# Hybrid layer on one core: where a new group's masked scores stand in TensorE's order

## The chip, the cores and the metric

The kernel runs on one core of a Trainium2 chip, as one launch. The metric is the time of one execution on the device in microseconds (us), as the median of the runs of a kernel. TensorE is called PE here, VectorE DVE, ScalarE ACT, GpSimd POOL and SyncE SP, as in the profile.

## The reference, cut to what matters

A layer with 1024 tokens (four batches of 256) and a width of 512: attention with an adapter, a clustered feed-forward layer, a state-space mixer and the feed-forward layer again, each on a layer-normalised input and added to the running `x`. The change lies in the mixer, which takes most of the time. It has 128 heads of 64 in eight groups of 16 heads:

```python
proj = input_states @ in_proj_w.T            # gate, then x, B, C, then dt
xBC = silu(causal_conv4(xBC) + conv_b)       # depthwise, four taps
dt = softplus(dt + dt_bias)
cum = cumsum(dt * A)
scores = (C @ B^T) * exp(cum_i - cum_j) * dt_j     # j <= i, heads of a group share B and C
y = scores @ x + D * x
g = y * silu(gate)
out = (g / rms of g over its group) * norm_w @ out_w.T
```

The products `C @ B^T` depend on the group and the batch only. They are computed and masked once for each group, and the 16 heads of the group multiply them with their own decay.

## The kernel before, in words

Channels lie on the 128 partitions, tokens along the free dimension. A block is 128 channels, which is two heads; there are 64 blocks, eight to a group. `block(i, ...)` (line 1175) is called once for each. Every product with weights is done as three matmuls on split operands (`mm3`, lines 110 to 117), so a projection of one block (1024 tokens) is two halves of 12 matmuls each, `projected` (line 1127), which calls `between` after the first half. What a block does:

- It projects its x channels into a PSUM tile `pp` and convolves them (`conv`, line 961): one scaling on ACT, three taps on DVE (line 971) that read PSUM, a SiLU on ACT (line 975). The result is `x2`.
- It projects its gate channels (also `pp`), with other PE work between the two halves, and ACT takes their SiLU (`gt`, line 1208).
- `differences` (line 999) makes the decays `em` of its two heads on DVE, POOL and ACT; `turned` (line 1022) transposes `x2` on PE into `trx` and scales it on DVE into `xd`; `weighted` (line 1019) multiplies each `em` with the group's masked scores `gm` on DVE (line 1020).
- `inner_products(i - 1)` (line 1160) does the weighted values of the block before: 32 matmuls into `pyy` (`product`, line 1038), then `gated` (line 1051): two steps on DVE (lines 1054 and 1057), a store to DRAM (`spill`), a square on ACT and its sum over the group on POOL (line 1067).
- `outer` (line 1150) does 24 matmuls (`pog`) of the output product of the group before, on what `recall` (line 1097) has loaded back from `spill` and split; the first of a group also takes the root of the summed squares (`root`, line 1085). `out_weights` (line 1073), eight a group, load and split the output weights: half of a group's before the gate projection of its last block, half at that block's end.

With the sixth and the seventh block of a group the B and C channels of the next group are projected and convolved. The first block of a group calls `scores` (line 978), a generator: it allocates `gm`, and each further step does two matmuls of one batch into a PSUM tile `pg` and one masking step on DVE (line 991) from there into `gm`. In every group but the first, the first block's order on PE is: both halves of x's projection; half of the gate's; scores of batches 0 and 1; weighted values of the block before; scores of batches 2 and 3; the other half of the gate's.

```python
for b in range(B):
    pg = ps.tile([P, 3, P], F32, name="pg", tag="m")
    ...
    nc.vector.tensor_tensor(gm[:, b], pg, tri.rearrange("p (s i) -> p s i", s=3), ALU.mult)
    yield
```

The tag "m" in `ps` has two buffers, which `pg`, `trx`, `pog` and the roots' `pqs` take by turns. `pp` has two buffers, `pyy`, `gm` and `xd` one, `em` four.

What sets the order: from block 8 on, PE's instructions stand in the order of the program (`manual_schedule`, line 1231). For the other engines the compiler's scheduler fixes an order ahead of time, the program's order being the priority among what it holds to be ready; at run time each engine works its list from the front. Nearly all DMAs are issued by SP.

Of the kernel before, what the change touches and what calls it, by code (L numbers as in the profile page):

```python
# [21 lines left out]
B, L, C = 4, 256, 512  # L22
# [57 lines left out]
def hybrid_kernel(  # L80
# [12 lines left out]
    x = keep.tile([P, TT, C], F32, name="x")  # L93
# [692 lines left out]
    def mixer(feed, later):  # L786
        with ExitStack() as es, ExitStack() as inner:
# [25 lines left out]
            def prepare(i):  # L813

                for n in range(i, i + 3):
                    fetch(n)
                if i < NW and i not in pieces:
                    pieces[i] = [pw.tile([P, KC, P], F32R, name=f"w{j}", tag=f"w{j}") for j in range(2)]
                    split(pieces[i], raws.pop(i), nc.gpsimd if i < 18 else nc.vector)

            def project(w, pp, cols):
                mm3(pp[:, cols], [[v[:, k, :] for v in w] for k in range(KC)],
                    [[v[:, k, cols] for v in xs] for k in range(KC)])
# [137 lines left out]
            def conv(pp, ch, tag, bufs):  # L961

                acc = (po_ if tag == "gb" else p2).tile([P, NT], F32, name="acc", tag=tag, bufs=bufs)
                nc.scalar.activation(  # L964
                    acc, pp, AF.Identity, bias=cb_s[:, ch : ch + 1], scale=cw_s[:, ch, 3:4]
                )
                av = acc.rearrange("p (b t) -> p b t", b=B)
                pv = pp.rearrange("p (b t) -> p b t", b=B)
                for tap in range(3):
                    d = 3 - tap  # L970
                    nc.vector.scalar_tensor_tensor(  # L971
                        av[:, :, d:], pv[:, :, : L - d], cw_s[:, ch, tap : tap + 1], av[:, :, d:],
                        ALU.mult, ALU.add,
                    )
                silus.append(nc.scalar.activation(acc, acc, AF.Silu).ins)
                return acc

            def scores(bt, ct):

                gm = p2.tile([P, B, 3, P], F32, name="gm", tag="gm", bufs=1)  # L980
                yield gm
                for b in range(B):
                    pg = ps.tile([P, 3, P], F32, name="pg", tag="m")
                    k0, k1 = bt[:, b * L : b * L + P], bt[:, b * L + P : (b + 1) * L]
                    q1 = ct[:, b * L + P : (b + 1) * L]
                    nc.tensor.matmul(
                        pg[:, 0:2, :].rearrange("p s i -> p (s i)"), k0, ct[:, b * L : (b + 1) * L],
                        start=True, stop=True,
                    )
                    nc.tensor.matmul(pg[:, 2, :], k1, q1, start=True, stop=True)  # L990
                    nc.vector.tensor_tensor(gm[:, b], pg, tri.rearrange("p (s i) -> p s i", s=3), ALU.mult)
                    yield

            def rows(h):
                r = p2.tile([P, NT], F32, name="r", tag="r", bufs=2)
                load(r, cumd[h : h + 1, :].to_broadcast([P, NT]))
                return r
# [21 lines left out]
            def weighted(e, gm):  # L1019
                nc.vector.tensor_tensor(e, e, gm, ALU.mult)  # L1020
# [52 lines left out]
            def out_weights(g, k):  # L1073

                r = po_.tile([P, C], F32, name="wor", tag="wor", bufs=2)
                tc.keep_in_program_order(load(r, wout[g * GB + k]))
                n = g * GB + k
                w = [po_.tile([P, C], F32R, name=f"wo{j}", tag=f"wo{j}", bufs=GB) for j in range(2)]
                nc.scalar.activation(w[0], r, AF.Copy, scale=nw_s[:, n : n + 1])
                nc.vector.scalar_tensor_tensor(  # L1080
                    w[1], r, nw_s[:, n : n + 1], w[0].bitcast(F32), ALU.mult, ALU.subtract
                )
                return w
# [43 lines left out]
            def projected(kind, n, between=lambda: None):  # L1127
                i = at[kind, n]
                prepare(i + 1)
                prepare(i + 2)  # L1130
                w = pieces.pop(i)
                if i == 0:
                    return first[1]
                pp = (
                    ps_y.tile([P, NT], F32, name="pp", tag="pyy") if (kind, n) == ("g", 0)
                    else ps_p.tile([P, NT], F32, name="pp", tag="pp")
                )
                for half in range(2):
                    project(w, pp, slice(half * 512, half * 512 + 512))
                    if half == 0:  # L1140
                        between()
                return pp
# [3 lines left out]
            def convolved(kind, g):  # L1146
                at_ = NB if kind == "b" else NB + G
                group[kind] = conv(projected(kind, g), at_ + g, "gb", 3)

            def outer():  # L1150

                q, t, hl = recalled.pop(0)
                po = ps.tile([P, C], F32, name="pog", tag="m")
                for half in range(2):
                    partial(po, q, hl[half], half)
                if t == 0:
                    rgs[q] = root(sqs.pop(q))
                scaled(q, t, po)

            def inner_products(m):  # L1160
                px2, gt, xd, em = stage.pop(m)
                py = product(xd, em)
                sqs[m // GB] = gated(m, px2, gt, py, sqs.get(m // GB))
# [2 lines left out]
            convolved("c", 0)  # L1166
            scoring = scores(group["b"], group["c"])
            gm = next(scoring)
            for _ in scoring:
                pass  # L1170
            rr = {h: rows(h) for h in range(2)}
            stage, sqs, wos, rgs, todo = {}, {}, {}, {}, []
            recalled = []
            PER = {1: 1, 2: 2, 3: 1, 4: 1, 5: 1, 6: 1, 7: 1}
            def block(i, scoring, gm):
                g, gi = divmod(i, GB)
                x2 = conv(projected("x", i), i, "x2", 2)
                if gi == 0 and g:
                    scoring = scores(group["b"], group["c"])
                    gm = next(scoring)  # L1180
                    todo.extend((g - 1, t) for t in range(TT))


                late = gi < 2 and g > 0
                if not late:
                    if recalled:
                        outer()
                    if i:
                        inner_products(i - 1)
                    while recalled:  # L1190
                        outer()
                if gi == 7:
                    wos.setdefault(g, []).extend(out_weights(g, k) for k in range(4))

                def between():
                    if late:
                        if gi == 0:
                            next(scoring)
                            next(scoring)
                        inner_products(i - 1)  # L1200
                        while recalled:
                            outer()
                    for _ in scoring:
                        pass

                pp = projected("g", i, between)
                gt = p2.tile([P, NT], F32, name="gt", tag="gt", bufs=1)
                nc.scalar.activation(gt, pp, AF.Silu)
                em = []
                for h in (2 * i, 2 * i + 1):  # L1210
                    with tc.issue_after(silus[2]) if i == 0 else ExitStack():
                        em.append(differences(h, rr.pop(h)))
                    if h + 2 < H:
                        rr[h + 2] = rows(h + 2)
                xd = turned(i, x2)
                if gi in NEXT and g + 1 < G:
                    convolved(NEXT[gi], g + 1)
                for e in em:
                    weighted(e, gm)
                stage[i] = (x2, gt, xd, em)  # L1220
                for _ in range(PER.get(gi + 1, 0)):
                    if todo:
                        q, t = todo.pop(0)
                        recalled.append((q, t, [recall(q, t, half) for half in range(2)]))
                if gi == 7:
                    wos[g].extend(out_weights(g, k) for k in range(4, 8))
                return scoring, gm

            for i in range(GB):
                scoring, gm = block(i, scoring, gm)  # L1230
            with tc.manual_schedule(engines={nc.tensor.engine}):
                for i in range(GB, NB):
                    scoring, gm = block(i, scoring, gm)
# [50 lines left out]

    later = ExitStack()
    mixer(attention(later), later)


# [67 lines left out]
```

## Time and profile before

| what | value |
|---|---|
| median of 3 runs | 1885.23 us (1880.72 to 1886.87) |
| the profiled execution | 1886.09 us |
| its span, first to last instruction | 1884.3 us |
| PE busy | 1805.5 us |
| DVE busy | 1475.8 us |
| ACT busy | 1470.4 us |
| masking steps (line 991) | 32, 0.55 us each (median) |
| products with the masked scores (line 1020) | 128, 1.75 us each (median) |
| mean granted clock of PE | 0.987 |

A row of the page's groups or of the timeline gives a line of the kernel, the engine, the operation, what it writes and reads, and how often; a time in square brackets is how long the engine stood idle before it, and for whom. "L1044" is line 1044. The profile gives one execution, with its own time; the runs' median comes from others.

### The profile page before, as it was taken

To read this page: it belongs to the slowest core of one execution; us is meant where nothing else is said; L and a number is where in the kernel's file an instruction comes from. 1 tells how busy PE (TensorE), PEld (TensorE's weight loads), DVE (VectorE), ACT (ScalarE), POOL (GpSimd) and SP (SyncE) were. 2 spreads that over 40 slices of the span, in tenths; PEclk is the share of its full clock that TensorE was granted. 3 is DMA by queue.
4 is the path that set the end of the run, shared out by engine and by line. 5 is a ranking of instruction groups with operands and counts; after the bars stand their busy time and mean duration, and the time that the engine had idled before them with its cause. 6 is when DMAs were issued, how large, how long until landed. Compare 5 with 4: busy or idle time off the path is not lost.

```text
span 1884.3 us, 29891 instructions
## 1 busy us (share of the span) xinstructions
PE 1805.5 (96%) x10706; PEld 1454.6 (77%) x10706; DVE 1475.8 (78%) x2304; ACT 1470.4 (78%) x2883; POOL 385.5 (20%) x393
## 2 busy tenths in 40 slices
PE   8999988899989999999999999999999999999997
PEld 6777767677777887878778878887887788788876
DVE  5566667789998788878887888779877978787777
ACT  6666675379998788878988798889788978887754
POOL 6332230014411211111112111111211111121100
PEclk9999999999999999999999999999999999999999
DMA  4000000034555445544554455445444544554241
GB/s 144 1 1 1 22 15 19 31 101 157 196 168 174 134 146 168 184 146 143 182 157 147 139 181 166 160 134 185 154 145 163 174 146 145 167 175 150 98 134 50
DMA packets 152773, 240.35 MB, mean 128 GB/s; under 512 B 12464, under 2 KB 77616, under 8 KB 152624
## 3 DMA queue, kind: packets, MB, share of 16 engines
q1 hardware_dynamic: 152624, 238.44, 39.0%
q8 instruction: 84, 1.38, 0.3%
q14 instruction: 65, 0.53, 0.1%
HBM read 202.75 MB, written 35.65 MB: 127 GB/s over the span
## 4 chain that ended last, share of the span: by engine, by line
PE 73%; DVE 12%; ACT 8%; DMA 3%; issue 3%; POOL 1%; SPq 0%; DVEq 0%; ACTq 0%; POOLq 0%
PE pp L115 11%; PE pp L116 11%; PE pp L117 11%; PE pyy L1044 7%; PE pog L115 6%; PE pog L117 6%; PE pog L116 6%; PE trx L1027 2%; ACT e L477 2%; DVE em L1020 2%; DVE acc L971 1%; DMA wor<-in_wout_dram 1%; PE ptr L493 1%; PE pq L115 1%; PE pq L116 1%
## 5 line engine op out<-in xcount | busy, mean ns | idle before, releaser
L115 PE MATMUL pp<-mx,w 128*128 128x512 f32 (+1 forms) x1160 | 464.2, 400 | 3.1 <-DVE acc L971 1.1
L116 PE MATMUL pp<-mx,w 128*128 128x512 f32 (+1 forms) x1160 | 453.1, 391 | 0.0
L117 PE MATMUL pp<-mx,w 128*128 128x512 f32 (+1 forms) x1160 | 452.8, 390 | 0.0
L971 DVE SCALAR_TENSOR_TENSOR acc<-pp,cw_s,acc 128x1012 f32<-128x1012 f32 (+2 forms) x240 | 304.8, 1272 | 21.3 <-ACT acc L964 19.4
L1020 DVE TENSOR_TENSOR em<-em,gm 128x1536 f32<-128x1536 f32 x128 | 249.2, 1952 | 54.6 <-ACT em L1016 54.6
L115 PEld LDWEIGHTS pp<-mx,w 128*128 128x128 f32 x1160 | 219.5, 189 | 53.7 <-issue 7.5
L1008 POOL TENSOR_SCALAR_AFFINE_SELECT r<-r 128x512 f32<-128x512 f32 x128 | 105.5, 825 | 749.0 <-DMA r<-cumd 616.5
L117 PEld LDWEIGHTS pp<-mx,w 128*128 128x128 f32 x1160 | 219.1, 189 | 46.6 <-issue 0.7
L116 PEld LDWEIGHTS pp<-mx,w 128*128 128x128 f32 x1160 | 219.4, 189 | 41.1 <-issue 0.6
L1067 POOL TENSOR_TENSOR sq<-sq,acc 128x1024 f32<-128x1024 f32 x55 | 139.0, 2528 | 359.7 <-ACT acc L1066 359.7
L115 PE MATMUL pog<-wo,gh 128*128 128x512 f32 x512 | 201.7, 394 | 1.3 <-DVE x L1115 0.8
L116 PE MATMUL pog<-wo,gh 128*128 128x512 f32 x512 | 199.6, 390 | 0.0
L117 PE MATMUL pog<-wo,gh 128*128 128x512 f32 x512 | 199.4, 390 | 0.0
L1044 PE MATMUL pyy<-em,xd 128*64 128x128 f32 (+1 forms) x2048 | 183.7, 329 | 1.3 <-DVE em L1020 0.9
L1044 PEld LDWEIGHTS pyy<-em,xd 128*64 128x64 f32 x2048 | 130.2, 137 | 59.8 <-issue 20.1
L1013 ACT ACTIVATE em<-r,col_t 128x128 f32<-128x128 f32 x512 | 170.1, 390 | 4.2 <-DMA r<-cumd 2.8
L1016 ACT ACTIVATE em<-r,col_t 128x128 f32<-128x128 f32 x512 | 169.2, 389 | 0.3
L1004 DVE TENSOR_SCALAR em<-r,col_t 128x128 f32<-128x128 f32 x512 | 135.7, 318 | 21.8 <-PE pyy L1044 17.8
L108 DVE TENSOR_TENSOR w<-wr,w 128x512 fp32r<-128x512 f32 x126 | 91.2, 724 | 76.8 <-ACT w L107 76.7
L107 ACT CAST w<-wr 128x512 fp32r<-128x512 f32 x144 | 88.7, 616 | 60.2 <-PE pp L116 57.4
L107 ACT CAST gh<-gr 128x512 fp32r<-128x512 f32 (+1 forms) x128 | 77.7, 608 | 62.7 <-PE pog L116 56.6
L477 ACT ACTIVATE e<-sc,nmx 128x256 f32<-128x256 f32 (+1 forms) x256 | 104.2, 442 | 21.0 <-DVE nmx L471 20.9
(290 smaller groups left out, 3309.0 us busy)
## 6 DMA issues: line engine op xcount, KB each, us to landing
wr<-in_win_dram SPq DMA_DIRECT2D x287, 256.0 KB, 2.8
r<-cumd SPq DMA_DIRECT2D x128, 512.0 KB, 4.0
spill<-gb SPq DMA_DIRECT2D x63, 512.0 KB, 2.8
gr<-spill SPq DMA_DIRECT2D x120, 256.0 KB, 2.9
wor<-in_wout_dram SPq DMA_DIRECT2D x64, 256.0 KB, 3.2
out_dram<-x SPq DMA_DIRECT2D x8, 256.0 KB, 2.3
x<-in_x_dram SPq DMA_DIRECT2D x1, 1536.0 KB, 8.8
gr<-spill SPq DMA_DIRECT2D x8, 192.0 KB, 2.5
```

Of the source, the lines that this page charges most:

```text
L107: nc.scalar.copy(hl[0], v)
L115: nc.tensor.matmul(o, lh, rh, start=(first and k == 0), stop=False)
L116: nc.tensor.matmul(o, lh, rl, start=False, stop=False)
L117: nc.tensor.matmul(o, ll, rh, start=False, stop=(last and k == n - 1))
L477: nc.scalar.activation(es_[c][:, 2 * j + pr, :], sc[:, j, :], AF.Exp, bias=nm[:, j : j + 1], accum_out=rs[:, c, h : h + 1],)
L971: nc.vector.scalar_tensor_tensor(av[:, :, d:], pv[:, :, : L - d], cw_s[:, ch, tap : tap + 1], av[:, :, d:], ALU.mult, ALU.add,)
L1004: nc.vector.tensor_scalar(e[:, b, 2, :], rv[:, b, 1, :], col_t[:, h, b, 1:2], 0.0, ALU.subtract, ALU.min,)
L1013: nc.scalar.activation(e[:, b, 1, :], rv[:, b, 1, :], AF.Exp, bias=col_t[:, h, b, 2:3])
L1016: nc.scalar.activation(e[:, b, 0, :], rv[:, b, 0, :], AF.Exp, bias=col_t[:, h, b, 0:1])
L1020: nc.vector.tensor_tensor(e, e, gm, ALU.mult)
L1044: nc.tensor.matmul(py[d, b, k * P :], xd[:, 2 * b + k, d], es2[hh][:, b, 2 * k : 2 if k == 0 else 3, :].rearrange("p s i -> p (s i)"), sta ...
L1067: (nc.gpsimd if n < NB - 1 else nc.vector).tensor_tensor(sq, sq, x2, ALU.add)
```

## The change

The generator's steps are no longer all taken between the halves of the gate's projection. In the first block of a group (not the first group) `scores` is now called before x's projection; a new local function `scored` takes two of its steps. It is passed to x's projection, so that scores of batches 0 and 1 stand between its halves, and with that ahead of x's convolution in the program, and it is called again at the head of `between`, so that scores of batches 2 and 3 stand in front of the weighted values of the block before. The four steps of group 0 are taken as before, by count.

```diff
--- before.py
+++ after.py
@@ -1166,19 +1166,25 @@
             convolved("c", 0)
             scoring = scores(group["b"], group["c"])
             gm = next(scoring)
-            for _ in scoring:
-                pass
+            for _ in range(B):
+                next(scoring)
             rr = {h: rows(h) for h in range(2)}
             stage, sqs, wos, rgs, todo = {}, {}, {}, {}, []
             recalled = []
             PER = {1: 1, 2: 2, 3: 1, 4: 1, 5: 1, 6: 1, 7: 1}
             def block(i, scoring, gm):
                 g, gi = divmod(i, GB)
-                x2 = conv(projected("x", i), i, "x2", 2)
                 if gi == 0 and g:
                     scoring = scores(group["b"], group["c"])
                     gm = next(scoring)
                     todo.extend((g - 1, t) for t in range(TT))
+
+                def scored():
+
+                    for _ in range(2 if gi == 0 and g else 0):
+                        next(scoring)
+
+                x2 = conv(projected("x", i, scored), i, "x2", 2)
 
 
                 late = gi < 2 and g > 0
@@ -1193,15 +1199,11 @@
                     wos.setdefault(g, []).extend(out_weights(g, k) for k in range(4))
 
                 def between():
+                    scored()
                     if late:
-                        if gi == 0:
-                            next(scoring)
-                            next(scoring)
                         inner_products(i - 1)
                         while recalled:
                             outer()
-                    for _ in scoring:
-                        pass
 
                 pp = projected("g", i, between)
                 gt = p2.tile([P, NT], F32, name="gt", tag="gt", bufs=1)
```

## The prediction

> **What bounds the kernel now.** I read first the page's busy times, then TensorE's (PE's) waits, then the timeline round one group start, then busy sums by window.
>
> ```profile
> span 1884.3 us, 29891 instructions
> ...
> PE 1805.5 (96%) x10706; PEld 1454.6 (77%) x10706; DVE 1475.8 (78%) x2304; ACT 1470.4 (78%) x2883; POOL 385.5 (20%) x393
> ```
>
> PE is busy in nearly all of the span. Summed over the stretch from 520 to 1700 us, its gaps of over 0.1 us come to only 18.7 us. PE's waits say whose they are (us in total, times, longest):
>
> ```profile
> PE pg L986 <- DVE gm L991: 14.4, 7, 4.6
> ...
> PE trx L1027 <- DVE gm L991: 2.1, 5, 1.0
> ...
> PE trx L1027 <- ACT rg L1093: 1.4, 1, 1.4
> ...
> PE trx L1027 <- DVE x L1115: 1.2, 4, 0.4
> ```
>
> Nearly all of it is one wait, seven times, once at each of the groups 1 to 7: the third batch's scores need a PSUM slot of the tag "m", which has two, and VectorE (DVE) has not yet masked the first batch's scores. PE's timeline at group 3 (start, us, what, idle before it):
>
> ```profile
> 912.56 0.59 PE L986 MATMUL pg<-acc 128*128 128x256 f32 x2
> ...
> 913.96 2.82 PE L1044 MATMUL pyy<-em,xd 128*64 128x256 f32 x32
> 918.28 0.70 PE L986 MATMUL pg<-acc 128*128 128x256 f32 x2 [1.51 <-DVE gm L991]
> ...
> 922.48 0.60 PE L1027 MATMUL trx<-con,acc 128*128 128x128 f32 x4
> ...
> 945.74 0.66 PE L1027 MATMUL trx<-con,acc 128*128 128x128 f32 x4 [0.23 <-DVE x L1115]
> ```
>
> DVE meanwhile, in the same window:
>
> ```profile
> 915.83 1.28 DVE L971 SCALAR_TENSOR_TENSOR acc<-pp,cw_s,acc 128x1020 f32<-128x1020 f32 x1
> 917.02 0.74 DVE L1080 SCALAR_TENSOR_TENSOR wo<-wor,nw_s,wo 128x512 fp32r<-128x512 f32 x1
> 917.68 1.02 DVE L991 TENSOR_TENSOR gm<-pg,tri 128x384 f32<-128x384 f32 x2
> 918.61 1.27 DVE L1054 SCALAR_TENSOR_TENSOR gb<-acc,dh,pyy 128x1024 f32<-128x1024 f32 x1
> ...
> 925.01 4.88 DVE L1020 TENSOR_TENSOR em<-em,gm 128x1536 f32<-128x1536 f32 x2
> ```
>
> The first two scores are ready at about 914, but their masks stand behind the convolution's taps and two output-weight splits and run at 917.68. The windows (length, then busy PE, PEld, DVE, ACT, POOL, and PE's granted clock) say what else is full:
>
> ```profile
> 903.50:911.50 8.00, 8.00 (x41) 6.77 (x40) 4.06 (x6) 7.96 (x12) 1.60 (x2) 1.00 0.61 222
> 911.50:925.10 13.60, 11.94 (x80) 9.54 (x79) 13.11 (x18) 12.35 (x20) 1.53 (x2) 1.00 0.65 212
> 925.10:945.70 20.60, 20.40 (x119) 16.41 (x117) 20.60 (x28) 19.06 (x32) 3.21 (x3) 1.00 0.61 192
> ```
>
> Before the scores DVE has 3.9 us to spare; from the first tap to the next block's transposes (945.7) it has 0.5 us, and the transposes wait 0.23 us for it. So PE and DVE share the limit there, and what PE gains DVE must match.
>
> **The change, part by part.** I work in group 3's clock. Scores of two batches take 1.35 us of PE, half a projection 2.73 (12 matmuls at 0.227), the weighted values (`product`) 2.75.
>
> 1. *The stall removed.* New PE order: x half 0 to 907.3, scores 0 and 1 to 908.6, x half 1 to 911.3, g half 0 to 914.0, scores 2 and 3 to 915.4, `product` to 918.1, g half 1 to 920.8, transposes of block 8. The number of PE instructions is the same. Masks 0 and 1 now have 5.4 us instead of 2.75, and stand ahead of the taps. Their slots come from block 7's transposes, read by DVE by 905.4, and the old mask tile was last read long before. So the whole stall goes: 1.51 here; 4.62, 1.47, 1.65, 1.52, 1.57 and 2.03 in groups 1, 2, 4, 5, 6 and 7, 14.4 in all. The small waits of the transposes for masks 2 and 3 in the same block (0.20, 0.15, 0.62, 0.15, 0.13) go too: 1.2.
>
> 2. *PE's clock.* Two of the stalls cost more than their length:
>
> ```profile
> 546.40:561.10 14.70, 10.08 (x62) 7.99 (x61) 11.49 (x16) 13.01 (x22) 1.37 (x2) 0.88 0.69 215
> 561.10:586.00 24.90, 23.10 (x136) 18.59 (x134) 22.68 (x35) 21.84 (x41) 4.60 (x4) 1.00 0.58 180
> 1630.00:1643.00 13.00, 10.97 (x69) 8.77 (x68) 11.67 (x15) 11.79 (x20) 1.07 (x2) 0.87 0.67 217
> ```
>
> A mean of 0.88 over 14.7 us is one stretch of 3.4 us at half clock, 1.7 us lost; so is the third row. The Trainium skill ("TensorE: Matmul & The Clock Gate", "HAM oscillation — how this bites in real kernels") says that only idle gaps above about 3.4 us throttle. By that rule only group 1's 4.62 does, and the stalls are worth 14.4 + 1.7 = 16.1. The trace differs: group 7's gap of 2.03 was followed by half clock, those of 1.5 were not. I follow the trace: 14.4 + 3.4 = 17.8, with the small waits 19.0. That is the ceiling.
>
> 3. *The convolution comes later.* The first pair of scores stands ahead of x's half 1, so x ends 1.3 us later, and ScalarE's (ACT's) first step, the taps and the SiLU with it. Before, SiLU ended at 920.17 and PE asked for it at 922.48: 2.3 us of cover. Now PE asks at 920.8, and a chain that is only shifted ends at 921.5: a new wait of 0.7. Masks 0 and 1 no longer matter to it: they run by 909.6, in DVE's idle time. Queued behind a DVE that waits for scores 0 would be weight splits that PE needs over 5 us later; that costs nothing.
>
> 4. *DVE's full stretch.* From the first tap to the end of the scaled transposes (911.53 to 925.09) the list is taps 3.57, five weight splits 3.35, one `w` split 0.60, four masks 1.9 (0.47 apart), gating 2.33, `xd` 1.20, idle 0.46. Now it starts at 912.84, without masks 0 and 1 (0.93) and with one weight split ahead of it (0.67): 11.4, so it ends at 924.2, 0.85 earlier. If the idle time stays and the split doesn't move: about 0.2 or below; if DVE also fills its gaps with the weighted rows, the 1.5 that PE gives. I take 0.9, since the list is the nearest thing to a row.
>    The two rows of weighted scores take 4.88 where two usual ones (1.75, median) take 3.42: the extra 1.46 lies beside GpSimd's square sum (924.21 to 926.6). The skill ("SBUF — State Buffer", "SBUF: two separate sides") says that whichever of the two starts first holds the port for the whole instruction. By that rule, a weighted row that starts before GpSimd's sum costs DVE nothing, and moving it could free 1.46; by the row it is hit in each of groups 2 to 6. The sum is fed by the gating, which also moves, so I leave the collision as it is: 0 on the path, up to 1.46 per group in the range.
>
> 5. *`product` later by 1.3.* Gating starts after 918.1 instead of at 918.61 (it had waited for masks): nothing. Its spill, the reload and the split for the first output product had 6.6 us to spare (split done 931.49, its matmul 938.06); at most 3 are used up. The weighted rows must be done before the next `product`: 929.9 against 932.0; PE comes 1.5 earlier and the rows 0.9: cover 1.5 of 2.1 left. SP's queue and the DMAs issue the same transfers in the same dependence, so I put them at nothing.
>
> **The sum.** Groups 2 to 6: 5 x 0.9 = 4.5. Group 7: PE gives 2.03 + 1.7; DVE's 0.85 plus idle 0.76 and 1.28 us in which it waited for PE's transposes allow 2.9; I take 2.9. Group 1: PE gives 6.3, but the next block's transposes already waited for ACT's root (1.36) and for DVE (0.44); ACT has 3.06 us idle in that stretch (24.9 less 21.84), so I take 3.0. Together 10.4. The profiled execution took 1886.09 us (span 1884.3 and 1.8 round it), 0.9 above the median of the runs shown; 1885.2 - 10.4 = 1874.8, so **1875 us**, 0.55% faster.
>
> **Rivals.**
> - *Everything keeps step.* DVE and ACT fill their gaps, the port collision dissolves: the ceiling, 19.0, 1866 us. For it: ACT has 1.2 us of idle waiting on DVE in each group, and an earlier mask leaves DVE more choice. Against: DVE's 20.60 busy of 20.60.
> - *The gain is given back.* The late SiLU and DVE's full stretch return it at the two transposes: 0.2 in five groups, 1 each in groups 1 and 7: 3 us, 1882.
> - *Slower: PE's wait moves from the scores to block 8's transposes.* x's convolution is now last to be ready. If in the new fixed order its taps or SiLU slip behind another weight split, masks 2 and 3 (0.93) and a table load (1.28), SiLU ends 2 us after PE asks, and such a gap (2.03 did) brings half clock: 3.7 per group. Against the stalls of now: +2.2 in five groups, -2.6 in group 1, 0 in group 7: +8.4, 1894. It decides from the point at which SiLU ends over 2.1 us later than now in the group's clock (1.3 is certain). Against it: DVE's order puts the taps ahead of masks 2 and 3.
>
> **How the numbers follow.** Chances: the likeliest case 0.47 (1870 to 1879.5), full gain 0.17 (1863 to 1870), given back 0.21, slower 0.15. A measurement of this kernel can tell about 0.3%, 5.7 us, from no change. Faster 0.64, same 0.21, slower 0.15. The range goes from 1865, inside the full gain, to 1888, over the case that gives back; left out are most of the slower case and the tail below.
>
> **What would show it.** PE's wait for `gm` at the scores should be gone from the list, masks 0 and 1 should run before the first tap, and the 0.88 and 0.87 clocks should be 1.00. Step 3 is right if block 8's transposes wait for ACT's SiLU by under 1 us; step 4 if the next block's transposes wait longer for the scaled output or the root than now (0.23), by about what PE gained and DVE didn't. The prediction is wrong upwards if transposes wait 2 us or more with half clock behind, or if the new order of ACT and DVE adds waits away from the group starts; downwards if the second transposes wait no longer than now.

## The result and the profile after

The changed kernel takes 1890.81 us (median of 6 runs, 1887.67 to 1894.86) against 1883.87 for the kernel before (6 runs): 1.0042 of it, 95% interval 1.0023 to 1.0061. Run again beside the experiments it took 1890.94 against 1885.35, 1.0031 (1.0021 to 1.0042). It is slower by 0.3 to 0.4%, where 0.55% faster was forecast. Its profiled execution took 1894.86 us.

The stall that the change aims at is gone. PE's waits in the changed kernel (whole span; us in total, times, longest):

```profile
PE pp L115 <- ACT gt L1210: 7.4, 8, 1.1
PE trx L1027 <- ACT acc L975: 5.6, 7, 1.3
...
PE pog L117 <- DVE gh L108: 2.5, 6, 0.5
```

No wait for `gm` at the scores is left. In its place PE waits for the SiLU of x's convolution (line 975), which the prediction had, and for the SiLU of the gate (line 1210 here, 1208 before) and the splits `gh`, which it had not. The wait for `gt` is at the gate projection of the second block of each group: it needs the PSUM tile `pp` that the gate of the first block still occupies. PE at group 3:

```profile
923.52 1.09 PE L1027 MATMUL trx<-con,acc 128*128 128x128 f32 x8 [0.64 <-ACT acc L975]
...
931.14 0.50 PE L115 MATMUL pp<-mx,w 128*128 128x512 f32 x1 [1.05 <-ACT gt L1210]
```

DVE shows why the gate's SiLU is late:

```profile
911.13 1.01 DVE L991 TENSOR_TENSOR gm<-pg,tri 128x384 f32<-128x384 f32 x2
...
919.76 1.27 DVE L971 SCALAR_TENSOR_TENSOR acc<-pp,cw_s,acc 128x1020 f32<-128x1020 f32 x1
920.95 1.01 DVE L991 TENSOR_TENSOR gm<-pg,tri 128x384 f32<-128x384 f32 x2
921.88 1.27 DVE L1054 SCALAR_TENSOR_TENSOR gb<-acc,dh,pyy 128x1024 f32<-128x1024 f32 x1
923.07 1.75 DVE L1020 TENSOR_TENSOR em<-em,gm 128x1536 f32<-128x1536 f32 x1
924.74 1.41 DVE L1080 SCALAR_TENSOR_TENSOR wo<-wor,nw_s,wo 128x512 fp32r<-128x512 f32 x2
926.07 1.22 DVE L1057 TENSOR_TENSOR gb<-gb,gt 128x1024 f32<-128x1024 f32 x1
```

Masks 0 and 1 run early, as they should. But with the last masks done before the gating, the first product with them (line 1020) is ready early too, and the scheduler has put it, and two output-weight splits behind it, between the two steps of the gating (1054 and 1057), in all seven groups. Before, a mask, a split and half a microsecond of idle time stood there:

```profile
919.80 0.55 DVE L991 TENSOR_TENSOR gm<-pg,tri 128x384 f32<-128x384 f32 x1
920.81 0.75 DVE L1080 SCALAR_TENSOR_TENSOR wo<-wor,nw_s,wo 128x512 fp32r<-128x512 f32 x1 [0.46 <-ACT wo L1079]
921.48 1.22 DVE L1057 TENSOR_TENSOR gb<-gb,gt 128x1024 f32<-128x1024 f32 x1
```

Counted from the start of the last block's transposes (903.5 before, 905.3 in this trace), the second step ends at 22.0 instead of at 19.2. ACT in the changed kernel, same window:

```profile
927.71 1.04 ACT L1066 ACTIVATE acc<-gb 128x1024 f32<-128x1024 f32 x1
928.77 1.28 ACT L1210 ACT_TABLE_LOAD   x1
930.07 1.02 ACT L1210 ACTIVATE gt<-pp 128x1024 f32<-128x1024 f32 x1
933.02 1.21 ACT L964 ACTIVATE acc<-pp,cb_s,cw_s 128x1024 f32<-128x1024 f32 x1 [1.94 <-POOL sq L1067]
```

and POOL:

```profile
928.90 4.09 POOL L1067 TENSOR_TENSOR sq<-sq,acc 128x1024 f32<-128x1024 f32 x1 [7.01 <-ACT acc L1066]
```

The square (line 1066) waits for the gating and stands ahead of the gate's SiLU, whose output `gt` has one buffer that the gating reads. And the square is written into the old `x2`, one of two buffers: the next block's convolution (line 964) can't start until POOL has summed it. That wait, ACT for POOL, comes to 12.1 us over seven groups in the changed kernel and doesn't occur in the kernel before. Most of it is the sum's own length: it takes 3.5 to 4.1 us here and 2.4 before.

A table of the ends of these steps, medians of groups 2 to 6, in us from the start of the last block's transposes (called the group's clock below):

| step | before | changed | gating first (below) |
|---|---|---|---|
| mask 0 | 14.7 | 6.2 | 5.3 |
| x's SiLU | 16.7 | 18.3 | 17.7 |
| weighted values (PE) | 13.3 | 14.6 | 14.6 |
| gating, first step | 16.4 | 18.0 | 17.3 |
| gating, second step | 19.2 | 22.1 | 18.7 |
| gate's SiLU | 22.9 | 25.9 | 21.3 |
| POOL's sum | 23.1 | 27.7 | 23.0 |

So of the 2.9 us by which the second gating step is later, 1.6 are a later start of the first, and 1.3 are the row and the splits where a mask and a split stood.

One caution for reading single traces. Up to block 8 the instructions stand in the same order in both kernels, yet the changed one reached block 7's transposes at 543.8 us against 540.0, and at 538.7 in its second trace; 13, 9 and 8 stretches at half clock lie ahead of that point. So I compare traces from those transposes to those of the last block: 1251.0 us before, 1254.8 and 1254.4 in the two traces of the changed kernel. That is 3.4 to 3.8 us, and the stretch behind the last transposes is 0.7 to 1.2 longer; the remaining 1 to 2 us of the medians' 5.6 to 6.9 these traces don't place.

### The profile page after: what moved, and what is told of

It is laid out like the page before. It is cut to its first block, busy times and chain, and to the rows that moved or that the text cites. A ratio compares the mean times of both kernels' runs of the same rounds, so it can differ in the third digit from the quotient of the medians.

```text
span 1893.1 us, 29893 instructions
## 1 busy us (share of the span) xinstructions
PE 1812.1 (96%) x10706; PEld 1454.0 (77%) x10706; DVE 1488.3 (79%) x2304; ACT 1479.3 (78%) x2897; POOL 396.4 (21%) x393
## 4 chain that ended last, share of the span: by engine, by line
ACT 34%; PE 25%; DVE 23%; issue 10%; DMA 6%; POOL 2%; SPq 0%; ACTq 0%; DVEq 0%; POOLq 0%
DVE acc L971 9%; ACT em L1013 4%; ACT em L1016 3%; ACT L1210 3%; ACT L1013 3%; ACT em L1014 2%; PE pp L115 2%; PE pp L116 2%; PE pp L117 2%; DVE gh L108 2%; ACT L1016 2%; ACT gt L1210 2%; ACT acc L964 2%; DMA gr<-spill 2%; ACT e L477 2%
## 5 line engine op out<-in xcount | busy, mean ns | idle before, releaser
L1020 DVE TENSOR_TENSOR em<-em,gm 128x1536 f32<-128x1536 f32 x128 | 243.1, 1900 | 110.3 <-ACT em L1016 104.7
L115 PEld LDWEIGHTS pp<-mx,w 128*128 128x128 f32 x1160 | 218.5, 188 | 64.2 <-ACT gt L1210 11.4
L1067 POOL TENSOR_TENSOR sq<-sq,acc 128x1024 f32<-128x1024 f32 x55 | 151.7, 2759 | 306.3 <-ACT acc L1066 306.3
L108 DVE TENSOR_TENSOR w<-wr,w 128x512 fp32r<-128x512 f32 x126 | 104.8, 831 | 34.9 <-ACT w L107 32.8
L115 PEld LDWEIGHTS pog<-wo,gh 128*128 128x128 f32 x512 | 96.1, 188 | 27.3 <-DVE xd L1030 2.7
```

The costliest lines, as they stand in the source:

```text
L108: engine.tensor_tensor(hl[1], v, hl[0].bitcast(F32), ALU.subtract)
L115: nc.tensor.matmul(o, lh, rh, start=(first and k == 0), stop=False)
L1067: (nc.gpsimd if n < NB - 1 else nc.vector).tensor_tensor(sq, sq, x2, ALU.add)
```

## The experiments

Theory A: the second gating step is pushed back by what the earlier masks let in front of it, and the next block waits for that. Theory B: x's convolution comes later, and everything else follows. Later a third, C: what counts is the load of DVE's list from the taps on, wherever a piece stands.

**The gating first.** In the changed kernel, the weighted rows of a group's first block are held behind the second gating step:

```diff
-                nc.vector.tensor_tensor(gb, gb, gt, ALU.mult)
+                gates.append(nc.vector.tensor_tensor(gb, gb, gt, ALU.mult).ins)
...
-                for e in em:
-                    weighted(e, gm)
+                with tc.issue_after(gates[-1]) if gi == 0 and g else ExitStack():
+                    for e in em:
+                        weighted(e, gm)
```

> The changed kernel, with the weighted rows of each group's first block held behind the second gating step (line 1057) on VectorE. Theory A (gating is pushed back by a weighted row and two weight splits, and with it the square, the gate's SiLU and the PSUM tile that the next block's gate projection waits for): that wait of TensorE (7.4 us over the groups, 1.05 each) goes, some 0.2 more each for refilling, so 7 to 9 us below the changed kernel, at about 0.999 to 1.001 of the kernel before. Theory B (x's convolution comes 1.3 us later, and everything late follows from that): under 2 us below the changed kernel, still about 1.003 to 1.004.

Measured: 1876.94 us, 0.9953 of before (0.9939 to 0.9967), 14.0 below the changed kernel on the same chip. B is out; A has the sign, and more than its 7 to 9. DVE at group 3:

```profile
914.21 1.27 DVE L1054 SCALAR_TENSOR_TENSOR gb<-acc,dh,pyy 128x1024 f32<-128x1024 f32 x1
915.39 0.28 DVE L1004 TENSOR_SCALAR em<-r,col_t 128x128 f32<-128x128 f32 x1
915.59 1.22 DVE L1057 TENSOR_TENSOR gb<-gb,gt 128x1024 f32<-128x1024 f32 x1
916.73 1.41 DVE L1080 SCALAR_TENSOR_TENSOR wo<-wor,nw_s,wo 128x512 fp32r<-128x512 f32 x2
918.05 1.28 DVE L1030 TENSOR_TENSOR xd<-trx,dt_t 128x512 f32<-128x512 f32 x2
```

Up to the first gating step the order is that of the changed kernel; behind it the two steps now follow each other, and the splits moved behind them too. PE's waits:

```profile
PE trx L1027 <- ACT acc L975: 5.6, 7, 2.0
PE trx L1027 <- DVE x L1115: 5.0, 6, 1.5
```

The waits for `gt` and for `gh` are gone, and ACT's for POOL. What is left is the late SiLU and the scaled output at the next block's transposes, both of which the prediction had. Where the time goes is read from the traces by blocks: the time from one block's transposes to the next block's, summed over groups 1 to 7, less that of the kernel before (us, half clock included; "only the first pair" is the third experiment):

| between the transposes of | changed | changed, second trace | gating first | only the first pair |
|---|---|---|---|---|
| a group's last block and the next group's first | -7.2 | -8.1 | -8.7 | -9.0 |
| the first and the second | +5.8 | +6.2 | -3.4 | -2.0 |
| the second and the third | +2.8 | +1.9 | +2.3 | -0.9 |
| all the rest | +2.4 | +3.4 | 0.0 | 0.0 |
| sum | +3.8 | +3.4 | -9.8 | -11.9 |

The change does gain at the scores. It loses most of that again between the transposes of the first and the second block, where the gate projection waits, and 9.2 of the 13.5 us that the gating first gives back lie there. The rest of the loss lies behind, part of it at output products of the fourth block (1.1 us of waiting for `xd`).

Two things this run doesn't settle. Which of the two, the row or the splits, does more of the delay isn't told apart. And ACT's order changed with it: no table load (1.28 us) stands between the square and the gate's SiLU any more, so SiLU ends 2.6 us behind the second gating step, where it was 3.8 in the changed kernel and 3.7 before. In all ACT makes 258 table loads, against 283 in the changed kernel and 269 before. Their number alone is not the cause: the kernel with the square later, below, has 256 and is still slower than the kernel before.

**The first pair behind x.** `x2 = conv(projected("x", i), i, "x2", 2)`, then `scored()`, in the changed kernel.

> The changed kernel, with scores of batches 0 and 1 behind both halves of x's projection instead of between them, so that x and its convolution come no later than before. Theory A: the wait of the next gate projection stays at about 1 us each, only the transposes' wait for SiLU (5.6 us over the groups) goes: 4 to 6 us below the changed kernel, about 1.001 to 1.002 of the kernel before. Theory B: nearly all waits behind the group starts go, 10 us or more below the changed kernel, 0.998 or less of the kernel before.

Measured: 1887.93 us, 1.0011 (1.0003 to 1.0019), 3.0 below the changed kernel. The wait for x's SiLU goes except in group 1 (3.9 us), the gate wait stays (4.6 over groups 1 to 7), but 4.5 us of waiting for masks at the scores come back and 4.4 for the scaled output. As A has it, and a little short of its 4 to 6: the late convolution is a small part of the loss.

**Only the first pair moved.** The first half of the change alone:

```diff
-                    scored()
                     if late:
                         inner_products(i - 1)
                         while recalled:
                             outer()
+                    scored()
```

> One part of the change alone: scores of batches 0 and 1 between the halves of x's projection, those of batches 2 and 3 behind the weighted values as before. Theory A: gating starts 1.3 us earlier than in the changed kernel and no weighted row stands in it, so the next gate projection doesn't wait; 7 to 9 us below the changed kernel, 0.999 to 1.001 of the kernel before, with the transposes' wait for SiLU still there (about 0.7 us each). Theory B: within 2 us of the changed kernel, about 1.003 to 1.004.

Measured: 1877.73 us, 0.9958 (0.9943 to 0.9973), 13.2 below the changed kernel, more than the 7 to 9 that A expected. So half of the change is worth 0.4% and the other half, scores 2 and 3 in front of the weighted values, costs 0.7 to 0.8%. Here the last masks come behind the gating's first step, so no weighted row can get in between, and the one wait that the prediction priced in step 3 leads the list of this stretch:

```profile
PE trx L1027 <- ACT acc L975: 5.3, 7, 2.2
```

**The changed kernel again.**

> The changed kernel once more, for a second trace and a narrower interval. Both theories: 1.002 to 1.006 of the kernel before; the stretches from block 8 to block 64 should come out as in its first trace (3.8 us longer than before), while the stretch ahead of block 8, whose orders are the same in both kernels, should not be 3.7 us longer again.

Measured: 1.0031 (1.0021 to 1.0042), and 1254.4 us from block 8 on. As expected.

**The square later.** In the changed kernel, square and sum are held in a list and emitted behind the gate's SiLU in a group's first block.

```diff
+                held = []
                 pp = projected("g", i, between)
...
                 nc.scalar.activation(gt, pp, AF.Silu)
+                for f in held:
+                    f()
```

> The changed kernel, with the square of the block before and its sum (ScalarE, GpSimd) held until behind the gate's SiLU in each group's first block; VectorE's gating keeps its place by the program. Theory A (the late second gating step holds ScalarE's square, which stands ahead of the SiLU that frees the next gate projection's tile): without the square (1.04 us) and with the table load (1.28) done while ScalarE waits, the SiLU comes some 2 us earlier, the wait of the gate projection (1.05 each) goes, 6 to 9 us below the changed kernel. Theory C (what costs is VectorE's order as a whole, taps and splits of the next block behind the gating): the gate projection's wait may go, but time moves under 3 us.

Measured: 1890.05 us beside 1886.57 for before, 1.0021 (1.0013 to 1.0030): about 2 us below the changed kernel's ratio. The wait for the gate is gone, as A said, but the time did as C said. The first row below shows where the gain went: the root (line 1098 here) became the last thing at the next block's transposes:

```profile
PE trx L1027 <- ACT rg L1098: 8.1, 7, 2.4
PE trx L1027 <- ACT acc L975: 3.5, 7, 1.1
PE trx L1027 <- DVE x L1120: 2.7, 6, 0.6
```

ACT's next convolution still waited for POOL's sum (2.6 us over the groups). DVE kept the changed kernel's order, with the row and the splits inside the gating, whose second step ended at 21.2 in the group's clock (22.1 in the changed kernel, 19.2 before). And since the square was held, the sum ended as late as in the changed kernel, 27.9 against 27.7. Freeing one thing that waits for the late gating doesn't free the others.

**The first pair behind x, the second behind the weighted values.** Both edits of the second and third experiment.

> Scores of batches 0 and 1 behind both halves of x's projection, those of 2 and 3 behind the weighted values as before: the kernel before with the first pair half a projection (2.7 us) earlier and its masks free to run ahead. Theory A: x's convolution is not late, so the transposes' wait for SiLU (5.3 us in the kernel with the first pair between the halves) goes, and no weighted row stands in the gating; 1 to 4 us below that kernel, 0.993 to 0.996 of the kernel before. Theory C (VectorE's list from the taps on is the limit): the wait only moves to the third batch's scores or the next block's transposes; 0.996 to 0.999.

Measured: 0.9965 (0.9952 to 0.9977), on C's side of the border, with an interval that reaches over it. The SiLU wait is gone and 6.2 us of waiting for the last masks at the transposes took its place.

**The first pair behind x, the gating first.**

> The changed kernel with scores 0 and 1 behind x's projection, and with the weighted rows held behind the second gating step. Theory A: neither the SiLU nor the gating is late; about 2 to 5 us below the kernel with the gating first alone, 0.992 to 0.995 of the kernel before. Theory C: the waits for the scaled output at the next block's transposes (5.0 us there) stay or grow, within 2 us of that kernel, 0.995 to 0.997.

Measured: 0.9962 (0.9947 to 0.9976), no better than the gating first alone, as C has it. Waits of 4.5 for the scaled output, 4.4 for masks at the scores, 2.1 for the root and, in group 1, 2.0 for SiLU. The late convolution isn't worth curing: what it gives PE is taken back at the next place where DVE's list is read.

**The delay put back by hand.** In the kernel with the gating first, for the last block of each group:

```diff
+                if n % GB == GB - 1 and n < NB - 1:
+                    for _ in range(2):
+                        nc.vector.tensor_tensor(gb, gb, ones, ALU.mult)
                 gates.append(nc.vector.tensor_tensor(gb, gb, gt, ALU.mult).ins)
```

(`ones` is broadcast to the shape.) And, as its counterpart, **the same work behind the weighted rows**: two such products on the second `em` tile of the block.

> The kernel with the gating first, and two more products with one (each about 1.2 us on VectorE, values unchanged) between its two gating steps for the last block of each group, seven times. The delay of the second step, about 2.4 us, is that of the changed kernel put back by hand. Theory A (the place of the gating is what costs): the waits behind it come back (ScalarE's first step of the next convolution on GpSimd's sum, the gate projection on the gate's SiLU, or the root), 1 to 2 us per group, 6 to 14 us above the kernel with the gating first, and clearly more than with the same work behind the weighted rows. Theory C (only the load of VectorE in this stretch counts): the same as with that work behind the weighted rows, within 2 us.

> The kernel with the gating first, and the same two products with one on VectorE in each group's first block, but on the weighted rows' own tile behind them instead of in the gating. Theory A: they cost what VectorE's list lacks before the next block's transposes, 0 to 1 us per group, 0 to 6 us above the kernel with the gating first. Theory C: 2 us and more per group, 12 us or more, the same as with them in the gating.

Measured: in the gating 1903.57 us, 1.0095 (1.0082 to 1.0108); behind the rows 1895.33, 1.0045 (1.0029 to 1.0061). PE's and ACT's waits with the delay in the gating:

```profile
PE pp L115 <- ACT gt L1216: 14.4, 9, 2.2
```

```profile
ACT acc L964 <- POOL sq L1073: 19.8, 7, 3.2
```

Both waits of the changed kernel are back and bigger. The added work is 2.5 us a group (two at 1.247), but the second gating step ends 4.1 later than with the gating first (22.8 against 18.7 in the group's clock), because two output-weight splits and half of `xd` went in front of it as well. So this is more than the changed kernel's delay (22.1). It makes the stretch from block 8 on 24.6 us longer, 3.5 a group; 10.2 of them are half clock, which came once in six of the groups (1.7 each; in group 1 behind a wait for x's SiLU). By the ratios the kernel is some 27 us above the one with the gating first, where A expected 6 to 14. With the work behind the rows:

```profile
PE pyy L1044 <- DVE em L1225: 14.4, 7, 2.9
```

The weighted rows are needed by the next `product`, and there is hardly any cover: PE waited for 14.4 of the 17.0 us of added work, and the stretch is 17.9 longer, 5.1 of it three stretches at half clock. My expectation for this run under A, 0 to 6 us, was wrong, and C's 12 or more was right. The two runs lie 8.2 us apart at the medians and 6.7 in the traces, and 5.1 of the 6.7 are the three more stretches at half clock. Without those the two cost nearly the same, so this pair doesn't show that a delay costs more inside the gating than elsewhere. It shows that DVE's list from the taps to the next weighted values has next to no slack. That the order of the list counts as well, with the same work in it, is shown by the gating first and by only the first pair moved.

**The weight splits behind the convolution.** In the kernel with only the first pair moved, the second half of `out_weights` is called behind the next block's `conv`.

> The kernel with only the first pair moved, and the second half of the output weights' loads and splits traced behind the convolution of the next group's first block instead of at the end of the block before. If what makes SiLU late at the transposes (5.3 us over the groups) is the splits between the taps, that wait shrinks by half or more and the kernel is 2 to 5 us faster than with only the first pair moved, 0.993 to 0.995 of the kernel before. If it is the projection's later end alone, the wait stays and the time is within 2 us.

Measured: 1.0035 (1.0022 to 1.0047), some 14 us slower than the kernel that it was to improve. The SiLU wait did shrink, from 5.3 to 1.3, and everything behind it grew:

```profile
PE trx L1027 <- DVE gm L991: 10.4, 8, 1.6
PE trx L1027 <- ACT rg L1093: 7.8, 6, 1.7
PE trx L1027 <- DVE x L1115: 5.8, 7, 1.0
```

(These three are of the whole span.) In every group one of the splits between the taps had moved to just ahead of the gating, and another in between the gating and the last mask. The expectation took the SiLU for the limit; it was only the first in line.

## Why the prediction was wrong

- *Step 1, the stall removed:* right. 14.4 us of waiting for `gm` became none. One thing was missed: in group 1 DVE was full before the scores too, and the scores of batch 0 waited 2.1 us for block 7's `xd`.
- *Step 2, the clock:* right in substance. From block 8 to the last block the kernel before had three stretches at half clock, the changed one had one and, in the second trace, none. The prediction counted two; the third follows two gaps of 1.36 and 0.44 us at the next transposes in group 1.
- *Step 3, the late convolution:* right, mechanism and size. A wait of 0.7 was forecast; 0.64 was measured at group 3, 5.6 over seven groups. (The splits between the taps have a part in it too: with one of them moved, the wait fell to 1.3.)
- *Step 4, DVE's full stretch:* this failed. The list from the first tap to the end of the scaled transposes was added up to 11.4 us, with its pieces in the old order, to end 0.85 earlier. At group 3 of the changed kernel it took 13.3, because a weighted row (1.7) now stood in it; it began 0.5 later than forecast, and it ended 1.6 us later than before in the group's clock. With the row held behind the gating the same list took 11.5, so the sum was right for an order that the scheduler didn't keep. The prediction did name the case "if DVE also fills its gaps with the weighted rows", but as its good end, worth 1.5; it was the case that came true.
- *The collision with POOL:* left in place by the prediction. It changed sides: in the changed kernel the second weighted row starts at 928.40, 0.5 us ahead of POOL's sum, and takes its usual 1.75, and the sum takes 4.09 instead of 2.4. That agrees with what the Trainium skill ("SBUF — State Buffer", "SBUF: two separate sides") says of the port, that the first to start holds it for its whole length; waiting for the row's end would account for 1.25 of the sum's extra 1.7 us. But what DVE was spared was put on the sum, for which the next convolution waited.
- *Step 5, `product` later by 1.3, "nothing":* the deciding failure. `product` ended where it was forecast, at 14.6 in the group's clock, but the gating's first step didn't start then: DVE came to it only behind the later taps and the masks of batches 2 and 3, 1.5 us later than before at group 3, where the prediction had it no later. Then the row and the splits stood in front of the second step. The prediction followed the gating to its spill and the first output product and found 6.6 us of cover, and it counted the weighted rows' cover. It didn't follow it to the square, to `gt`'s one buffer with the PSUM tile behind it, and to the buffer of `x2` that POOL's sum gives back. There the cover was gone: 1.05 us of waiting at the gate projection in most groups. With the gating kept together, `product` comes just as much later and the second step still ends 0.5 earlier than before: so the price was not of the later `product` but of what DVE did between it and the end of the gating.
- *The rivals:* the slower one was given 0.15 and ended at 1894. The sign came true, its mechanism didn't: x's SiLU ended 1.6 us later in the group's clock, short of the 2.1 that it needed, and PE waits at the transposes of a group's first block by 0.2 to 1.3 us, not by 2. The loss is at the next gate projection and at later output products. The prediction's other sign of being wrong upwards, that "the new order of ACT and DVE adds waits away from the group starts", comes nearest to what was seen.
- *The sum:* 10.4 us faster was forecast. With the gating first, which is near the kernel that the sum described, the gain is 8.4 us at the medians (1885.35 to 1876.94), in the form forecast: late SiLU, and a longer wait for the scaled output. That the totals come so close is in part luck: ACT's order is another one there, and by groups the traces have a gain of 5.5 in group 1 (3.0 forecast), 0.7 in group 7 (2.9), and between a gain of 1.2 and a loss of 0.2 in groups 2 to 6 (0.9 each).

## What to carry to other kernels

When a change makes a value ready earlier, list what consumes it: under a scheduler that fills gaps by readiness, the consumer can move forward too, and land in front of something that was on time. Follow a delayed step to every buffer that it frees, not only to the data that it writes; here a scratch write into another tile's buffer tied POOL's sum to the next convolution. And a half of a change can be worth more than the whole: moved alone, the first pair of scores gave 0.4%; pinning one order made the whole worth 0.5%.

## What the runs showed of the hardware

PE's clock drops after less idle time than the rule weighed in the prediction has it, and not always after the same gap. A gap of 2.1 us at group 1's scores stands in eight of the traces; half clock followed it in two of them. The traces show why. In each trace every stretch at half clock starts on one grid of 3.413 us (to within 4 ns), and whether half clock follows goes with how much of such a window PE was idle, which depends on where a gap falls. From block 7's transposes to the last block's the twelve traces have 4395 windows. Half clock followed all 14 in which PE was idle for 1.91 us or more, none with 1.76 or less, and 2 of the 7 between. The first pair of rows is a window in the changed kernel and the one behind it, the second a pair with the gating first (length, busy PE, PEld, DVE, ACT, POOL, then PE's granted clock):

```profile
543.30:546.71 3.41, 1.55 (x11) 0.98 (x9) 3.41 (x11) 3.39 (x5) 0.29 (x1) 1.00 0.66 202
546.71:550.12 3.41, 3.16 (x10) 2.70 (x11) 2.78 (x6) 2.52 (x7) 0.00 (x0) 0.50 0.32 109
```

```profile
556.57:559.98 3.41, 1.56 (x7) 0.94 (x5) 3.41 (x6) 3.38 (x7) 0.00 (x0) 1.00 0.74 236
559.98:563.40 3.42, 3.29 (x19) 2.85 (x20) 3.22 (x6) 3.42 (x6) 1.39 (x2) 1.00 0.69 277
```

Both first windows are idle for 1.9 us, just over half, which is the border: the first was followed by half clock, the second wasn't. Two gaps of 1.36 and 0.44 us in one window were enough in the kernel before, while its gaps of 1.5 at the scores were not. The matmuls' ends are modelled in the trace, so this border is a rough one.
